# Second layer of a two-layer vision state-space kernel: batch by batch, or stage by stage over all batches

## The chip, the cores and the metric

The kernel runs on one core of a Trainium2 chip. The metric is the device time of one execution in microseconds (us). The engines go by short names: PE is TensorE (matmul; PEld is its weight load), DVE is VectorE, ACT is ScalarE, POOL is GpSimd, SP is SyncE, which issues most DMAs.

## The reference, cut to what matters

The input is `x` with 4 batches of 64x64 positions (L = 4096) and 192 channels, in float32. Two layers follow one another; each adds its result to its input. Both normalise the input by groups, project it to 2x384 channels, run selective scans in four directions over the positions, normalise over channels, multiply by a gate and project back to 192. The change is in the second layer:

```python
xz = x @ W_in
x_val, z = (xz[..., :D_INNER], xz[..., D_INNER:])
xc = conv_general_dilated(xc, conv_w, padding='SAME', feature_group_count=D_INNER)  # 3x3, per channel
xc = silu(xc + conv_b)
y = y1 + y2 + y3 + y4          # scans of rows, rows reversed, columns, columns reversed
y = (y - mu) * rsqrt(var + 1e-05) * gamma + beta
y = y * silu(z)
return y @ W_out

def _ssm_scan(u, ...):         # one direction, 16 states n per channel
    dt = softplus(dt @ W_dt + b_dt)
    log_decay = cumsum(dt * A)
    decay = exp(log_decay)
    h = decay * cumsum(dB_u / (decay + 1e-12))
    return einsum('bldn,bln->bld', h, C_mat) + u * D_param
```

Because of the `1e-12`, a state's output dies away after some steps from where its scan starts. The kernel computes only the first 256 steps of state 0, 128 of states 1 to 3, 64 of states 4 to 7 and 32 of states 8 to 15, in each of the four directions, and tests on the way that this is enough (`alive`); a general layer stands behind it for the case that it isn't, and is not entered here. The rest of y is `4*D*u`, for all 4096 positions.

## The kernel before, in words

`two_layer_vmamba` runs the first layer for each of the four batches (`layer.run(x[b], mid[b])`), then the second layer for each (`layer.run(mid[b], out[b])`). Positions go in 8 tiles of 512 (NCH = 8, LC = 512), inner channels in 3 blocks of 128 (ND = 3). The two layers share `norm` (L442 to L486), `in_proj` (L488, matmuls at L490) and `finish` (from L853). One run of the second layer has three parts.

`project` first normalises (L454 to L482, PE transposes and small DVE work). Then, for each channel block e, ACT copies eight projected tiles into a padded 66x66 plane (`pad`, L993), and each half of the plane (128x2048) is convolved: the middle row of three taps on PE with diagonal weights (L1005), the first tap joined with it from PSUM by DVE in quarters of the half, and five taps (1, 2, 6, 7, 8) on DVE over the whole half (L1023, `acc`). ACT's silu (L1031) writes `u`. GpSimd copies the ends of the plane to `uc` (L1042 rows, L1045 columns), the 512 positions near the four starts and the 512 after these. At last, tile by tile, the gate half of the projection is copied out (L1051) and stored, and `u` is transposed on PE (L1060), multiplied by 4·D on DVE (L1061) and stored to `y` in DRAM.

`scans` works on four items: M (first 128 steps of each direction, states 0 to 3), E (the next 128 steps, state 0), S and Q (64 and 32 steps, states 4 to 7 and 8 to 15). A preparation computes dt (ACT Exp and Ln, POOL L1121 to L1125, DVE L1128), its running sums (L1132 `cum`), dt·u transposed (L1187), and the rows of B and C. Nine steps follow; a step makes 128x1536 values of `h`: `weight` (ACT, Sigmoid of the sums, L1237), `decay` (ACT, Exp, L1250), `b_product` (ACT, L1272), `turn_x` (PE, L1287), `scan` (DVE, L1294 and L1132), `c_product` (POOL, L1310) and, two steps later (LAG = 2), `add_y` (PE, L1328, sums in PSUM) or `ext_y` for E (L1344, L1345). `store` adds M's and E's sums into `y` by accumulating DMAs that POOL issues (L1364, L1367). The order in this part is written out by hand (`manual_schedule`) for PE, ACT, DVE and POOL: each takes its instructions in the order of the text, so a waiting instruction holds all behind it on its engine. Elsewhere a scheduler orders the instructions by their data and by free buffers.

`finish` goes tile by tile: loads of `y`, gate and input; statistics per position (DVE L874), their root (ACT L877, which needs a table of its own), scaling (DVE L880), transposes (PE L887), gamma and beta (ACT L890), the product with silu of the gate (DVE L893), the output matmul (PE L898), the input added (DVE L901), and the store.

Of the kernel before, what the change touches and what calls it, by code (L numbers as in the profile page):

```python
# [23 lines left out]
NX = 64  # L24
# [378 lines left out]
class FirstLayer:  # L403
# [29 lines left out]
    def run(self, src, dst):  # L433
        with self.tc.tile_pool(name="xT", bufs=1) as px:
            self.xT = px.tile([CB, NC2, L], F32, name="xT")
            self.w_in = px.tile([CB, NC2, 2 * DI], F32, name="w_in")
            self.bias = px.tile([128, 2 * ND], F32, name="bias")
            self.project(src)
            self.scans()
        self.finish(src, dst)  # L440
# [412 lines left out]
    def finish(self, src, dst):  # L853
        nc, tc = self.tc.nc, self.tc
        with ExitStack() as ctx:
            pool = lambda name, bufs, **k: ctx.enter_context(tc.tile_pool(name=name, bufs=bufs, **k))
            pl, pw = pool("fl", 3), pool("fw", 2)
# [4 lines left out]
            for t in range(NCH):  # L862
                pos = lambda a: a[t * LC : (t + 1) * LC, :].rearrange("(j p) c -> p j c", p=128)
                yt = pl.tile([128, NJ, DI], F32, name="yt")
                nc.sync.dma_start(yt, pos(self.y_dram))
                zg = pl.tile([128, ND, LC], F32, name="zg")
                nc.sync.dma_start(zg, self.gate[t])
                nc.scalar.activation(zg, zg, AF.Silu)
                xl = pl.tile([128, NJ, CH], F32, name="xl")
                nc.sync.dma_start(xl, pos(src))  # L870
                st = pw.tile([128, NJ, nc.vector.BN_STATS_DIM], F32, name="st")
                mv = pw.tile([128, NJ, 2], F32, name="mv")
                for j in range(NJ):
                    nc.vector.bn_stats(st[:, j, :], yt[:, j, :])  # L874
                    nc.vector.bn_aggr(mv[:, j, :], st[:, j, :])
                rs = pw.tile([128, NJ], F32, name="rs")
                nc.scalar.activation(rs, mv[:, :, 1], AF.Sqrt, bias=self.ln_eps)  # L877
                nc.vector.reciprocal(rs, rs)
                for j in range(NJ):
                    nc.vector.tensor_scalar(  # L880
                        yt[:, j, :], yt[:, j, :], mv[:, j, 0:1], rs[:, j : j + 1], ALU.subtract, ALU.mult
                    )
                v = pw.tile([128, ND, LC], F32, name="v")
                for d in range(ND):
                    vp = pm.tile([128, LC], F32, name="vp")
                    for j in range(NJ):
                        nc.tensor.transpose(  # L887
                            vp[:, j * 128 : (j + 1) * 128], yt[:, j, d * 128 : (d + 1) * 128], self.ident
                        )
                    nc.scalar.activation(  # L890
                        v[:, d, :], vp, AF.Identity, bias=self.beta[:, d : d + 1], scale=self.gamma[:, d : d + 1]
                    )
                nc.vector.tensor_mul(v, v, zg)  # L893
                ot = pw.tile([128, NJ, CH], F32, name="ot")
                for j in range(NJ):
                    op = po.tile([128, CH], F32, name="op")
                    for d in range(ND):
                        nc.tensor.matmul(  # L898
                            op, v[:, d, j * 128 : (j + 1) * 128], w_out[:, d, :], start=(d == 0), stop=(d == ND - 1)
                        )  # L900
                    nc.vector.tensor_add(ot[:, j, :], op, xl[:, j, :])  # L901
                nc.sync.dma_start(pos(dst), ot)


class SecondLayer(FirstLayer):
# [4 lines left out]

    CLASSES = ((0, 1, 2 * SEG), (1, 4, SEG), (4, 8, SEG // 2), (8, 16, SEG // 4))

    def __init__(self, tc, ctx, consts, w, gate, bc_pool, y_dram, alive):
        nc = tc.nc
        self.tc, self.w, self.alive = tc, w, alive
        self.ident, self.group, self.one = consts
        self.gate, self.bc_pool, self.y_dram = gate, bc_pool, y_dram
# [33 lines left out]
    def run(self, src, dst):  # L951
        tc = self.tc
        with tc.tile_pool(name="uc", bufs=1) as pc:
            self.uc = pc.tile([128, 2, ND, LC], F32, name="uc")
            with tc.tile_pool(name="u", bufs=1) as pu:
                self.u = pu.tile([128, ND, L], F32, name="u")
                self.project(src)
            self.scans()
        self.finish(src, dst)


    def project(self, src):
        nc, tc = self.tc.nc, self.tc
        with ExitStack() as ctx:
            pool = lambda name, bufs, **k: ctx.enter_context(tc.tile_pool(name=name, bufs=bufs, **k))
            px, pl, ps = pool("xT", 1), pool("ld", 3), pool("st", 1)
# [3 lines left out]
            pd, pc, pa = pool("dg", 2), pool("pad", 2), pool("acc", 2)  # L970
            dsum = ps.tile([128, DI], F32, name="dsum")
            nc.sync.dma_start(dsum, self.w["D_rows"][0].partition_broadcast(128))
            nc.vector.tensor_scalar_mul(dsum, dsum, float(KD))
            self.xT = px.tile([CB, NC2, L], F32, name="xT")
            self.w_in = ps.tile([CB, NC2, 2 * DI], F32, name="w_in")
            self.bias = bias = ps.tile([128, 2 * ND], F32, name="bias")
            self.norm(src, pl, ps, pt)
            in_proj = lambda e, t: self.in_proj(pm.tile([128, LC], F32, name="pp"), e, t)


            rows = LC // HW
            half = NCH // 2
            for e in range(ND):
                dg = pd.tile([128, 3, 128], F32, name="dg")
                for dx in range(3):
                    nc.vector.tensor_scalar_mul(dg[:, dx, :], self.ident, self.cw[:, e, 3 + dx : 4 + dx])
                pad = pc.tile([128, HW + 2, HW + 2], F32, name="pad")
                nc.gpsimd.memset(pad[:, 0, :], 0.0)  # L988
                nc.gpsimd.memset(pad[:, HW + 1, :], 0.0)
                nc.gpsimd.memset(pad[:, 1 : HW + 1, 0:1], 0.0)  # L990
                nc.gpsimd.memset(pad[:, 1 : HW + 1, HW + 1 : HW + 2], 0.0)
                for t in range(NCH):
                    nc.scalar.activation(  # L993
                        pad[:, 1 + t * rows : 1 + (t + 1) * rows, 1 : 1 + HW],
                        in_proj(e, t).rearrange("p (h w) -> p h w", w=HW),
                        AF.Identity,
                        bias=bias[:, e : e + 1],
                    )
                for q in range(2):
                    acc = pa.tile([128, half * rows, HW], F32, name="acc")  # L1000
                    for t in range(half):
                        cp = pm.tile([128, rows, HW], F32, name="pp")
                        r0 = q * half * rows + t * rows
                        for dx in range(3):
                            nc.tensor.matmul(  # L1005
                                cp,
                                dg[:, dx, :],
                                pad[:, 1 + r0 : 1 + r0 + rows, dx : dx + HW],
                                start=(dx == 0),
                                stop=(dx == 2),  # L1010
                            )
                        nc.vector.scalar_tensor_tensor(
                            acc[:, t * rows : (t + 1) * rows, :],
                            pad[:, r0 : r0 + rows, 0:HW],
                            self.cw[:, e, 0:1],
                            cp,
                            ALU.mult,
                            ALU.add,
                        )
                    r0 = q * half * rows  # L1020
                    for tap in (1, 2, 6, 7, 8):
                        dy, dx = divmod(tap, 3)
                        nc.vector.scalar_tensor_tensor(  # L1023
                            acc,
                            pad[:, r0 + dy : r0 + dy + half * rows, dx : dx + HW],
                            self.cw[:, e, tap : tap + 1],
                            acc,
                            ALU.mult,
                            ALU.add,
                        )  # L1030
                    nc.scalar.activation(  # L1031
                        self.u[:, e, q * half * LC : (q + 1) * half * LC],
                        acc.rearrange("p h w -> p (h w)"),
                        AF.Silu,
                        bias=self.cb[:, e : e + 1],
                    )
            v = self.u.rearrange("p d (h w) -> p d w h", w=HW)
            for r in range(2):
                near, far = r * SEG, (r + 1) * SEG
# [25 lines left out]
    def scans(self):  # L1065
        nc, tc = self.tc.nc, self.tc
        with ExitStack() as ctx:
# [93 lines left out]
            def test(it):  # L1161

                for i, (_, _, n) in enumerate(self.CLASSES):
                    if (n > SEG) != it.r:
                        continue
# [390 lines left out]
```

## Time and profile before

| | |
|---|---|
| median of 3 runs | 11613.56 us (11609.38 to 11620.19) |
| profiled execution, its own time | 11625.22 us |
| its span, first to last instruction | 11623.4 us |
| granted TensorE clock, mean | 0.930 |
| busy in the span | PE 85%, PEld 64%, DVE 84%, ACT 83%, POOL 74% |
| DMA | 1213.58 MB, mean 104 GB/s |
| ACT table loads in the second layer's scans | 8 of Sigmoid (L1237), 1283 ns each |
| second layer | 9916.3 to the end, four batches of about 425.6 us |

The first layer takes 9916 of the 11623 us, so the shares of the whole span describe it more than the second layer. A row of the groups of instructions reads: line, engine, operation, output <- inputs by the program's names, shapes, count, then busy time in us with the mean ns of one, then the idle time before them with what ended it. A row of the timeline reads: start in us, duration, engine, line, operation, names, shape, count, and in brackets the wait before it with what ended it.

### The profile page before, as it was taken

What the parts mean: (1) busy time and instruction counts of PE and PEld (TensorE: products, weight loads), DVE (VectorE), ACT (ScalarE), POOL (GpSimd) and SP (SyncE); (2) the same over time, 40 slices, a digit from 0 to 9 for tenths busy, and PEclk for the clock granted to TensorE, in tenths of its full rate; (3) what the DMA queues carried; (4) which work ended last, traced back from release to release, by engine and by line L of the source; (5) the groups of instructions that cost most, each with busy time, mean ns of one, the idle gap of its engine ahead of it and who ended that gap; (6) DMA issues with size and microseconds to landing.
All of it is one profiled execution on the core that took longest, in us unless ns stands there. A gap on an engine that the chain in (4) does not pass through costs nothing. (4 is left out here: it accounts for less than half of the span.)

```text
span 11623.4 us, 171905 instructions
## 1 busy us (share of the span) xinstructions
PE 9831.9 (85%) x61689; PEld 7403.8 (64%) x61689; DVE 9803.3 (84%) x12067; ACT 9634.3 (83%) x16710; POOL 8590.2 (74%) x2840
## 2 busy tenths in 40 slices
PE   7998888878988888789988888789888887876876
PEld 4776666656776666657766666567766666454454
DVE  4999899957999899849998999679998998666655
ACT  5999999948999999859999999589999998345435
POOL 3999899927999899739998999279998997112112
PEclk8999999988999999989999999889999999887888
DMA  4333343443333343433333444433333344233123
GB/s 124 107 105 99 93 102 97 97 144 113 108 101 95 96 102 97 130 120 109 106 100 93 98 101 98 143 112 110 100 97 96 99 99 125 72 91 126 60 88 124
DMA packets 738067, 1213.58 MB, mean 104 GB/s; under 512 B 48538, under 2 KB 439719, under 8 KB 737204
## 3 DMA queue, kind: packets, MB, share of 16 engines
q1 hardware_dynamic: 732340, 1196.21, 37.0%
q0 software_dynamic: 4864, 6.29, 0.4%
q8 instruction: 490, 8.03, 0.3%
q14 instruction: 373, 3.06, 0.1%
HBM read 927.26 MB, written 275.09 MB: 103 GB/s over the span
## 5 line engine op out<-in xcount | busy, mean ns | idle before, releaser
L738 POOL TENSOR_TENSOR h<-h,bct 128x1536 f32<-128x1536 f32 x2048 | 7065.1, 3473 | 581.0 <-DVE carry L734 481.3
L724 DVE TENSOR_TENSOR_SCAN h<-a,carry,x 128x512 f32<-128x512 f32 x5376 | 6606.0, 1267 | 230.6 <-PE x L716 188.2
L716 PE MATMUL x<-ident,xT 128*128 128x128 f32 x24576 | 4002.5, 287 | 814.5 <-DVE h L724 711.9
L699 ACT ACTIVATE xT<-dtuT,bT 128x384 f32<-128x384 f32 x8192 | 4356.6, 608 | 92.8 <-PE x L716 88.6
L716 PEld LDWEIGHTS x<-ident,xT 128*128 128x128 f32 x24576 | 2804.5, 145 | 2139.3 <-DVE h L724 927.8
L711 ACT ACTIVATE a<-dt,A_log_f 128x512 f32<-128x512 f32 x6144 | 3975.4, 715 | 0.0
L751 PE MATMUL yp<-ident,h 128*128 128x128 f32 x24576 | 3704.7, 277 | 9.2 <-POOL h L738 9.2
L751 PEld LDWEIGHTS yp<-ident,h 128*128 128x128 f32 x24576 | 2945.7, 144 | 78.5 <-issue 62.6
L615 PE MATMUL dp<-xd,w_dtb_f 13*128 13x512 f32 x1536 | 890.4, 663 | 208.5 <-DVE dt L644 207.5
L724 DVE TENSOR_TENSOR_SCAN h<-a,x 128x512 f32<-128x512 f32 x768 | 899.2, 1207 | 193.2 <-PE x L716 116.7
L628 POOL TENSOR_SCALAR wl<-e 128x1536 f32<-128x1536 f32 x128 | 189.5, 1481 | 950.1 <-ACT e L624 791.2
L490 PE MATMUL pp<-xT,w_in 96*128 96x512 f32 x1152 | 544.6, 620 | 0.0
L615 PEld LDWEIGHTS dp<-xd,w_dtb_f 13*128 13x128 f32 x1536 | 238.9, 192 | 453.6 <-DVE dt L644 336.2
L745 PE MATMUL yp<-yold,ident 128*128 128x512 f32 x768 | 442.0, 660 | 72.9 <-DMA yold<-y 72.9
L988 POOL MEMSET pad<- 128x66 f32 x12 | 2.1, 172 | 678.0 <-DVE acc L1023 660.5
L621 ACT ACTIVATE e<-dp 128x512 f32<-128x512 f32 x384 | 225.0, 586 | 309.9 <-DVE dt L644 153.9
L641 POOL TENSOR_TENSOR e<-e,wl 128x1536 f32<-128x1536 f32 x128 | 445.6, 3481 | 0.3
L638 POOL TENSOR_TENSOR e<-e,dt 128x1536 f32<-128x1536 f32 x128 | 443.4, 3464 | 0.3
L898 PE MATMUL op<-w_out,v 128*128 128x192 f32 x1536 | 321.7, 378 | 112.7 <-DVE v L893 112.7
L898 PEld LDWEIGHTS op<-w_out,v 128*128 128x128 f32 x1536 | 307.5, 226 | 125.5 <-DVE v L893 125.5
L734 DVE TENSOR_REDUCE carry<-h 128x3 f32<-128x3 f32 x2048 | 322.7, 158 | 70.4
L490 PEld LDWEIGHTS pp<-xT,w_in 96*128 96x128 f32 x1152 | 222.2, 199 | 248.6 <-issue 243.3
(188 smaller groups left out, 7217.9 us busy)
## 6 DMA issues: line engine op xcount, KB each, us to landing
bct<-xp SPq DMA_DIRECT2D x1024, 512.0 KB, 4.9
y<-du SPq DMA_DIRECT2D x64, 768.0 KB, 5.2
uT<-uT SPq DMA_DIRECT2D x64, 768.0 KB, 4.9
yold<-y SPq DMA_DIRECT2D x64, 768.0 KB, 7.9
gate<-zg SPq DMA_DIRECT2D x64, 768.0 KB, 5.6
y<-yt SPq DMA_DIRECT2D x64, 768.0 KB, 4.2
uT<-uT SPq DMA_DIRECT2D x128, 384.0 KB, 5.1
yold<-y SPq DMA_DIRECT2D x128, 384.0 KB, 5.5
```

The costliest lines, as they stand in the source:

```text
L490: self.tc.nc.tensor.matmul(pp, self.w_in[:, i, e * 128 : (e + 1) * 128], self.xT[:, i, t * LC : (t + 1) * LC], start=(i == 0), stop=(i == ...
L615: nc.tensor.matmul(self.dp[d], w, self.xd[0 : DR + 1, :], start=True, stop=True)
L638: nc.gpsimd.tensor_tensor(self.e, self.e, self.dt, ALU.subtract)
L641: nc.gpsimd.tensor_tensor(self.e, self.e, self.wl, ALU.add)
L699: nc.scalar.mul(xTs[g][:, j, :], it.dtuT[:, j * DI : (j + 1) * DI], it.bT[:, j, n : n + 1])
L711: nc.scalar.activation(as_[g][:, d, :], it.dt[:, d, :], AF.Exp, scale=scale)
L716: nc.tensor.transpose(xs[g, d][:, j * 128 : (j + 1) * 128], xTs[g][:, j, d * 128 : (d + 1) * 128], ident)
L724: nc.vector.tensor_tensor_scan(along(hs[g][:, d, :], it.k), along(as_[g][:, d, :], it.k), along(xs.pop((g, d)), it.k), 0.0 if it.first els ...
L738: nc.gpsimd.tensor_tensor(hs[g], hs[g], bc(cs[g - n % 2][:, n % 2, :], 1, ND), ALU.mult)
L745: nc.tensor.matmul(it.yp[b], ident, yo, start=True, stop=False, skip_group_check=True)
L751: nc.tensor.matmul(it.yp[b][:, i * 128 : (i + 1) * 128], hs[g][:, d, j * 128 : (j + 1) * 128], ident, start=False, stop=n == NS - 1, is_tr ...
L898: nc.tensor.matmul(op, v[:, d, j * 128 : (j + 1) * 128], w_out[:, d, :], start=(d == 0), stop=(d == ND - 1))
```

## The change

- `SecondLayer.run` takes all four batches. Each of its stages goes through all batches before the next stage begins: `project`, `prepare`, `scans`, `finish`. `y` and the gate have a DRAM buffer for each batch, and `uc` goes to DRAM as well.
- `project`: the middle-row taps leave PE. ACT makes taps 0 and 1 (Identity with a scale, 128x2048), POOL adds them, DVE does taps 2 to 8. The normalisation of the next batch is placed after the second channel block of the present one. `uc` is copied by POOL for each half-plane and direction, six copies per half. `4·D·u` comes from a PE matmul of `u` with a diagonal matrix, copied by ACT and stored in blocks of 128 channels (runs of 512 bytes). The gate is stored per channel block.
- `prepare` is new: for M and E of each batch it computes dt, sums and dt·u, cuts S and Q out of M on POOL, and keeps all in DRAM.
- `scans` is one pipeline of 4x9 = 36 steps, with the loads of the next batch's items at its steps 0, 3, 5 and 6. The Sigmoid weights come in two bursts for each batch, five after step 3 and four after step 8. A batch's sums are copied out and stored at step 2 of the next.
- `finish` takes a list of batches: all eight tiles of `y` are loaded and their statistics computed first, with one root for the whole batch; those of the next batch are placed after tile 4. The product with the gate's silu moves from DVE to POOL. The first layer uses this form too, one batch at a time.

The diff, cut:

```diff
...
-    def run(self, src, dst):
...
+    def run(self, batches):
...
+        self.prepare(ucs, chunks)
+        self.scans(chunks, [y for _, _, y, _ in batches])
+        self.finish(batches)
...
+                        nc.scalar.activation(acc, part(0), AF.Identity, scale=weight(0))
+                        nc.scalar.activation(u, part(1), AF.Identity, scale=weight(1))
+                        nc.gpsimd.tensor_tensor(acc, acc, u, ALU.add)
+                        for tap in range(2, 9):
+                            nc.vector.scalar_tensor_tensor(acc, part(tap), weight(tap), acc, ALU.mult, ALU.add)
+                        nc.scalar.activation(u, acc, AF.Silu, bias=self.cb[:, e : e + 1])
...
+                            nc.gpsimd.tensor_copy(to, u[:, row : row + n, :])
...
+                                nc.gpsimd.tensor_copy(to[:, :, q * nh : (q + 1) * nh], wide[:, col : col + n, :])
...
+                                nc.tensor.matmul(
+                                    dq[:, j, :], flat[:, at : at + 128], self.dg[:, e, :], start=True, stop=True
+                                )
+                            du = pl.tile([128, NJ, 128], F32, name="du")
+                            nc.scalar.copy(du, dq)
...
+                    if e == 1 and b + 1 < len(batches):
+                        ready = normed(batches[b + 1][0])
...
+                    burst = {3: range(g + 1, g + 6), 8: range(g + 1, g + 5)}.get(n, ())
...
+                    if n == LAG and b > 0:
+                        end_y(b - 1)
+                        if g < N:
+                            start_y()
...
+                for t in range(NCH):
+                    yt = py.tile([128, NJ, DI], F32, name="yt")
+                    nc.sync.dma_start(yt, pos(y, t))
...
+                        nc.vector.bn_stats(st[:, j, :], yt[:, j, :])
...
-                nc.vector.tensor_mul(v, v, zg)
...
+                    nc.gpsimd.tensor_tensor(v, v, zg, ALU.mult)
...
+                    if t == NCH // 2 and b + 1 < len(batches):
+                        ready = stats(batches[b + 1][2])
...
```

## The prediction, made before the changed kernel ran

> **What bounds the kernel now.** I read first the per-core view (one core, span 11623.4 us, clock 0.930), then the timeline for where the second layer starts: its first statistics begin at 9916.3, and its four batches follow one another at about 425.6 us each. Only this last 1707 us and the output stage of the first layer are touched. So the page's shares over the whole span decide nothing here, and I cut the first batch of the second layer into stages. The columns are the stretch, its length, busy us of PE, PEld, DVE, ACT and POOL, then PE clock, DMA share and GB/s.
>
> ```profile
> 9916.00:9950.00 34.00, 22.63 (x95) 16.18 (x96) 13.86 (x30) 10.79 (x18) 0.00 (x0) 0.57 0.24 70
> 9950.00:10061.00 111.00, 111.00 (x256) 48.89 (x257) 76.34 (x54) 28.29 (x32) 3.38 (x12) 0.98 0.00 0
> 10061.00:10108.00 47.00, 45.96 (x175) 24.62 (x174) 26.13 (x37) 18.55 (x25) 5.38 (x8) 1.00 0.65 245
> 10108.00:10157.00 49.00, 30.62 (x72) 13.71 (x73) 25.93 (x41) 27.20 (x37) 24.84 (x20) 0.61 0.12 40
> 10157.00:10230.00 73.00, 43.27 (x269) 34.71 (x268) 58.57 (x114) 54.55 (x119) 28.66 (x9) 0.79 0.10 27
> 10230.00:10270.00 40.00, 17.65 (x133) 14.88 (x130) 2.65 (x8) 7.50 (x6) 13.80 (x20) 0.77 0.57 128
> 10270.00:10342.00 72.00, 50.11 (x289) 47.17 (x289) 54.68 (x145) 39.52 (x47) 0.00 (x0) 0.84 0.71 236
> ```
>
> The rows are norm, convolution, gate with D·u, scan preparation, scan steps, the scan's tail with its stores, and output. Convolution is bound by PE (111.00 of 111.00). The tail of 40 us has no busy engine: it is a chain of waits. The other stages have no full engine either. Then the durations, from the groups of instructions with forms apart:
>
> ```profile
> L898 PE MATMUL op<-w_out,v 128*128 128x192 f32 x1536 | 321.7, 378 | 112.7 <-DVE v L893 112.7
> L1023 DVE SCALAR_TENSOR_TENSOR acc<-pad,conv_w_s,acc 128x2048 f32<-128x2048 f32 x120 | 281.1, 2351 | 1.3
> L893 DVE TENSOR_TENSOR v<-v,zg 128x1536 f32<-128x1536 f32 x64 | 112.1, 1752 | 28.5 <-ACT v L890 27.7
> L1132 DVE TENSOR_TENSOR_SCAN cum<-keep_s,dt 128x256 f32<-128x256 f32 x24 | 45.3, 1927 | 0.4
> ```
>
> Last the timeline, for what the scan's tail waits on. POOL issues the accumulating stores of the E chunk one by one, each waiting for the one before to land, and the last h·C product stands behind them:
>
> ```profile
> 10228.30 1.06 POOL L1364 DMA_DIRECT2D y<-yte  x1 [0.61 <-ACT yte L1345]
> 10232.69 1.70 POOL L1367 DMA_DIRECT2D y<-yte  x2 [3.33 <-DMA y<-yte]
> 10237.02 0.90 POOL L1364 DMA_DIRECT2D y<-yte  x1 [2.63 <-DMA y<-yte]
> 10240.84 1.68 POOL L1367 DMA_DIRECT2D y<-yte  x2 [2.92 <-DMA y<-yte]
> 10241.96 4.00 POOL L1310 TENSOR_TENSOR h<-h,bct 128x1536 f32<-128x1536 f32 x1
> ```
>
> So one store set holds POOL for about 14.2 us (10228.3 to 10242.5).
>
> **What the Trainium skill says.** (1) "SBUF — State Buffer", section Who interferes with whom: a DVE instruction with two SBUF inputs and a GpSimd instruction that reads SBUF share a read port, and the second to issue waits until the first is done. The trace agrees. The 128x256 scan takes 674 ns in the main loop (L1132 h) but 1927 on average where POOL works beside it (row above). In the timeline:
>
> ```profile
> 10132.06 3.67 POOL L1123 TENSOR_TENSOR e<-e,dt 128x1536 f32<-128x1536 f32 x1
> 10133.13 6.92 DVE L1132 TENSOR_TENSOR_SCAN cum<-keep_s,dt 128x256 f32<-128x256 f32 x2
> 10135.81 3.68 POOL L1125 TENSOR_TENSOR e<-e,wl 128x1536 f32<-128x1536 f32 x1
> 10140.66 1.27 DVE L1132 TENSOR_TENSOR_SCAN cum<-keep_s,dt 128x256 f32<-128x256 f32 x2
> ```
>
> Two scans take 6.92 beside POOL and 1.27 alone; two products of 3.42 and two scans of 0.63 make 8.1, and 8.0 pass from 10132.06 to 10140.05. The port is handed over whole, at no extra price. (2) "GPSIMD Engine Reference", section 4.1 Engine selection: two-input elementwise work is about twice as slow as on VectorE; the trace has 3510 against 1752 ns for 128x1536. (3) "ScalarE: Activation LUTs", section What ACT_TABLE_LOAD costs: about 1.28 us a load plus a drain; the load is 1283 ns here, and no drain is seen after it.
>
> **The change, part by part.** P, S, C, O are its four stages.
>
> *P, norm to gate, now for all batches in a row.* Before: 34+111+47 = 192 per batch, 768. After, PE has 192 projection passes at 0.461 (88.5), 192 D·u passes of 128 columns, about 0.15 each (29), and norm (22.6): 140 per batch; the 144 convolution passes (62.4) are gone. ACT has 24 pad copies and 24 gate copies at 0.69 (33), 12 Identity passes of 128x2048, not in the trace, bounded by the silu of that size, 2.0 (24), 6 silus (12), 24 du copies at 0.59 (14), norm 11: about 95, hidden. DVE has 7 taps of 2.351 for each half-plane (taps read two SBUF inputs), 6 half-planes: 98.7. With norm (11) and small work (2), 112. On top come GpSimd's holds of the shared port: six adds of 128x2048, 3473×2048/1536 = 4.63 each, of which five fall between taps (23); and 36 copies to uc, 12 at 0.40 and 24 of 64x32 pieces, no row, nearest the 404 ns of 128x128, taken 0.29 (between 0.2 and 1.5), about 10 between taps. That makes **145 per batch**. DVE is now the bound, just above PE. At each turn of a batch pads come only after the last silu: bias products 4, four pads 5, ACT taps and add 9, in all 19 us, three times. Start: norm 34 and 16 to the first tap. End: 12. SP issues 24 D·u and 24 gate stores per batch instead of 8 and 8, and the next batch's norm loads stand behind them; the same bytes moved in 47 us before and have 145 now, so nothing, with 10 per batch as the cost if the loads come late. P = 50+3×145+134+57+12 = **about 690, −78**. Bounds: 560 if the port costs DVE nothing (PE's 4×140), 830 if each half-plane pays as in the rival below.
>
> *S, prepare, all batches ahead of the scans.* Before 49 per batch (196). After, the chain of one batch is read from the same rows: xd to exp 8.7 with a table load, POOL 10 (2×1.5+2×3.5), delta and sums 6.3, then for the second chunk wl, dt and two products behind POOL's part copies (15), sums 7, products and transposes to dtuT 6: 53. The next batch's Abs stands behind this batch's dtuT copies on ACT, so 7+4×53 = **219, +23**. Chunks stored to DRAM, 6.5 MB per batch, take 20 us at 332 GB/s (236/0.71 of the output row) and lie under the 53. Bounds 170 (if batches overlap) and 260.
>
> *C, one pipeline of 36 steps.* Before 73+40 per batch (452). ACT's work per batch is 26.3 weights (105.3/4), 21.8 decays, 19 b products, 2.4 copies, 5.1 table loads: 74.6. The drain and fill, paid four times now, are paid once. But the E store still holds POOL 14.2 us, and in the pipeline it starts just after the weights of the ninth step: product 8 waits, add_y 8 follows about 9 later on PE, and ACT's copy of ytm stands ahead of the next burst: about 12 of stall. Period 86.5. Load 6, ramp 54, three periods 259: 320 to the last batch's final steps, with the y loads of O starting meanwhile, 47 after that. C = **320**. Bounds: 284 (no stall), 368 (twice the stall).
>
> *O, output for four batches.* Before 72 each (288). After: 76 to 78 us from the end of those 320 for the first y loads, behind the last stores, and all eight statistics; first tile 16; then 32 tiles. A tile moves 2.36 MB, 7.1 us at 332 GB/s. PE needs 5.6 to 6.8. DVE has 1.75 less (row L893), but the product goes to POOL at 3.5 and holds the port there: about 7.3. So O = 78+16+32×7.25+6 = **332, +44**. The skill, (4) "DMA: Bandwidth & Descriptors", section Where 436 GB/s comes from, gives about 358 GB/s as the HBM limit of a core; the trace shows 236 at share 0.71, and I use that. C and O together take 652 against 740: −88.
>
> *First layer's output, four times.* Its stage is 84 us (9832 to 9916). All eight tiles' statistics now go first: PE starts near +29 instead of +10, then runs 5.8 to 6.4 per tile. **+6 each, +24**; bounds −10 (POOL's product frees DVE) and +45.
>
> Table loads: in O and in the first layer's output 100 become 17, in prepare 16 come new; off the bounding engine in both, so nothing. If ACT were the bound, 83×1.28 = 106.
>
> Sum for the second layer: 690+219+320+332 = 1561 against 1707 (3 more than my rounded stages add up to), −146; with +24, −122. The profiled execution took 11625.2 by its own time (span 11623.4), so 11503; the median of the runs is 11.7 below the profiled one: **11492 us**. What is late next: in P DVE, in C ACT with POOL's stall, in O the DMA.
>
> **The rivals.** (R1) Faster: DVE doesn't wait for GpSimd in P, which is PE-bound at 560. −130 more: 11362. Against it stands the 1927 ns row. (R2) Slower than before: the port in P. Each half-plane has seven GpSimd instructions (one add, six copies), and DVE and GpSimd take turns. If a half-plane costs 30 us instead of 24, because each of the seven holds the port 0.9 longer than its own length or the 64x32 copies take 1.3 to 1.5, P grows by 24×6 = 144: 11636. It decides from 5.1 us per half-plane upward (122/24). For it: the copies' strided form has no row. Against it: the 8.0 us hand-over shows no extra price. (R3) Faster: POOL's store stall is not on the path of C, period 74.6, −36: 11456. (R4) No change: the pipeline does not do what it says, because loads of the next batch come late or batches of S and O wait for DRAM; the gain of C and O goes (88) and a little of P: 11590 to 11620.
>
> **How the numbers follow.** Forecast 0.54, R1 0.10, R3 0.10, R4 0.08, R2 0.18 (with all other sums that end slower). A measurement here can tell about 0.2% (23 us) from no change. Faster: 0.54+0.10+0.10 = 0.74; same 0.08; slower 0.18. The range reaches from 11380, which leaves out most of R1 (0.07), to 11620, which takes in R4 and leaves out 0.13 of R2. Its width is that of P's bounds for the most part.
>
> **What would show it.** Right: taps of 128x2048 near 2.35 with one or two per half-plane near 4 to 7; a half-plane every 24 us; prepare with a period near 53; sigmoid bursts 86 apart; output tiles 7.2 apart at a DMA share near 1; first statistics 29 ahead of PE in the first layer's output. Wrong: half-planes at 30 or more (R2) or P ending at 560 (R1), a period of 75 (R3), scan groups waiting on DMA loads (R4).

## The result, and the profile after

The changed kernel takes 11564.99 us (median of 4 runs, 11548.21 to 11574.44) against 11613.05 for the kernel before in the same comparison: a ratio of 0.9956, with a 95% interval of 0.9939 to 0.9974. It is faster, by 48 us. The prediction said 11492, faster by 122. The direction was right, and the time lies in the range; the gain is 0.4 of the forecast.

The profiled execution of the changed kernel took 11574.44 us (span 11572.7), 50.8 less than that of before. First the stages, in the view by stretches (columns as in the prediction). The rows are norm; the first batch of convolution and gate; the first batch of prepare; a period of the scan pipeline; then the last stores, the statistics, and the first two stretches of the output stage.

```profile
9948.00:9998.00 50.00, 34.99 (x120) 21.66 (x121) 13.52 (x26) 17.45 (x25) 0.90 (x8) 0.69 0.38 112
9998.00:10160.00 162.00, 123.41 (x474) 72.39 (x473) 123.91 (x68) 89.03 (x110) 85.07 (x54) 0.86 0.34 111
10633.00:10687.00 54.00, 34.64 (x68) 14.68 (x68) 10.52 (x32) 19.25 (x23) 26.75 (x24) 0.59 0.31 115
...
10983.00:11068.00 85.00, 56.82 (x388) 45.52 (x386) 52.34 (x91) 71.89 (x146) 41.20 (x21) 0.84 0.48 121
11240.00:11268.00 28.00, 8.80 (x66) 7.42 (x63) 1.69 (x3) 7.39 (x6) 5.18 (x6) 0.68 0.73 208
11268.00:11300.00 32.00, 7.11 (x37) 6.55 (x38) 26.51 (x91) 4.44 (x7) 7.98 (x2) 0.61 0.79 290
11300.00:11366.00 66.00, 47.98 (x273) 44.99 (x272) 54.08 (x142) 30.34 (x34) 30.63 (x8) 0.89 0.71 238
11366.00:11433.00 67.00, 52.78 (x302) 49.14 (x302) 47.39 (x123) 31.79 (x37) 26.71 (x8) 0.87 0.77 255
```

In a convolution batch of 162 us PE and DVE are both busy for 124 and ACT for 89: no engine is full. The output stage has no full engine either, and DMA is at 0.71 to 0.77. Both are chains of waits. The groups of instructions of the changed kernel name what is waited for:

```profile
L912 PE MATMUL op<-w_out,v 128*128 128x192 f32 x1536 | 302.0, 364 | 105.9 <-POOL v L907 104.3 <-DVE ot L915 1.5
L907 POOL TENSOR_TENSOR v<-v,zg 128x1536 f32<-128x1536 f32 x64 | 238.2, 3742 | 422.2 <-ACT v L904 380.3 <-ACT zg L888 35.8 <-PE vp L901 6.0
L1056 DVE SCALAR_TENSOR_TENSOR acc<-pad,conv_w_s,acc 128x2048 f32<-128x2048 f32 x168 | 446.2, 2702 | 139.1 <-POOL acc L1054 138.8
L1054 POOL TENSOR_TENSOR acc<-acc,u 128x2048 f32<-128x2048 f32 x24 | 134.6, 5608 | 130.9 <-ACT u L1053 130.9
L1053 ACT ACTIVATE u<-pad,conv_w_s 128x2048 f32<-128x2048 f32 x24 | 47.9, 1997 | 65.8 <-POOL uc L1067 61.2 <-PE pp L490 4.6
L1067 POOL COPY uc<-u 128x64 f32<-128x64 f32 x96 | 103.7, 1107 | 0.0
L1064 POOL COPY uc<-u 128x128 f32<-128x128 f32 x48 | 102.7, 2139 | 181.6 <-ACT u L1057 181.6
L939 DVE TENSOR_TENSOR_SCAN cum<-keep_s,dt 128x256 f32<-128x256 f32 x24 | 14.4, 666 | 0.0
```

PE's output matmuls waited for DVE's product before (112.7 in both layers) and wait about as long for POOL's now. The taps are longer (2702 against 2351 ns), and DVE stands idle for 139 us until POOL's add. POOL itself stands idle for 131 us before its adds, until ACT's second tap (L1053) is done. POOL's copies of 128x128 (columns before, rows now) take 2139 ns against 404. In exchange the running sums in prepare (`cum`) have the port for themselves: 666 ns against 1927.

E's stores still stand ahead of a batch's last product. After them three products follow in one run, and PE's sums (L1343) wait for the first of these:

```profile
11057.71 0.91 POOL L1377 DMA_DIRECT2D y<-yte  x1 [8.06 <-ACT yte L1361]
11061.87 1.69 POOL L1380 DMA_DIRECT2D y<-yte  x2 [3.25 <-ACT a L1267]
11066.22 0.90 POOL L1377 DMA_DIRECT2D y<-yte  x1 [2.66 <-ACT a L1267]
11070.99 1.68 POOL L1380 DMA_DIRECT2D y<-yte  x2 [3.87 <-DMA y<-yte]
11072.12 10.77 POOL L1325 TENSOR_TENSOR h<-h,bct 128x1536 f32<-128x1536 f32 x3
11076.17 3.42 PE L1343 MATMUL yp<-ident,h 128*32 128x128 f32 x16 [5.62 <-POOL h L1325]
```

The timeline gives all stages to a microsecond, and the same instants can be read in each experiment. "Start" is the first transpose of the second layer's norm; "conv" runs from there to the last gate copy; "prepare" to the last copy of dt·u; "scans" from the first to the last product of x; "output" from the first output matmul to the last sum.

| run | median us | start | conv | prepare | scans | output |
|---|---|---|---|---|---|---|
| changed kernel | 11565.0 | 9952.6 | 680.0 | 237.1 | 323.2 | 268.2 |
| e1 product on DVE | 11445.3 | 9888.9 | 676.9 | 235.3 | 324.4 | 211.1 |
| e2 four v | 11567.3 | 9946.7 | 680.1 | 236.4 | 324.9 | 273.8 |
| e3 first layer's old form | 11530.4 | 9909.1 | 678.4 | 235.1 | 326.3 | 268.3 |
| e4 store late | 11540.1 | 9935.5 | 679.7 | 236.9 | 300.3 | 263.5 |
| e5 no add | 11541.1 | 9940.6 | 662.3 | 236.5 | 326.2 | 265.8 |
| e6 copies on ACT | 11543.3 | 9944.2 | 656.9 | 235.5 | 325.2 | 268.7 |
| e7 e5 and e6 | 11445.7 | 9941.2 | 565.8 | 234.8 | 324.3 | 262.0 |
| e8 ytm apart | 11560.2 | 9943.7 | 676.4 | 237.0 | 325.2 | 279.4 |
| e9 six PSUM banks | 11578.6 | 9942.1 | 674.6 | 238.2 | 324.3 | 283.6 |
| e10 prepare in pairs | 11560.8 | 9950.9 | 679.9 | 229.1 | 325.6 | 267.3 |
| e13 PE's order | 11507.3 | 9926.9 | 677.0 | 238.3 | 321.8 | 235.6 |
| e14 no add, borders on DVE | 11428.4 | 9939.2 | 538.8 | 244.8 | 323.9 | 261.7 |
| e16 borders on DVE | 11534.1 | 9935.0 | 663.7 | 231.5 | 324.7 | 268.6 |

The start varies from run to run: in the eight runs that leave all of `finish` as changed (e4 to e8, e10, e14, e16) it lies between 9935.0 and 9950.9, mean 9941. So the changed kernel's profile, with 9952.6, is late by some 11 us, and differences of ten microseconds in the median of a run are read from the stages here.

### The profile page after: what moved, and what is told of

The parts are those of the page before. It is cut to its first block, busy times and chain, and to the rows that moved or that the text cites. A ratio compares the mean times of both kernels' runs of the same rounds, so it can differ in the third digit from the quotient of the medians.

```text
span 11572.7 us, 172113 instructions
## 1 busy us (share of the span) xinstructions
PE 9631.2 (83%) x61497; PEld 7333.9 (63%) x61497; DVE 9684.7 (84%) x11675; ACT 9692.9 (84%) x16786; POOL 9137.6 (79%) x3024
## 5 line engine op out<-in xcount | busy, mean ns | idle before, releaser
L907 POOL TENSOR_TENSOR v<-v,zg 128x1536 f32<-128x1536 f32 x64 | 238.2, 3742 | 422.2 <-ACT v L904 380.3
L1056 DVE SCALAR_TENSOR_TENSOR acc<-pad,conv_w_s,acc 128x2048 f32<-128x2048 f32 x168 | 446.2, 2702 | 139.1 <-POOL acc L1054 138.8
```

What stands on the lines that cost most here:

```text
L1056: nc.vector.scalar_tensor_tensor(acc, part(tap), weight(tap), acc, ALU.mult, ALU.add)
```

## The experiments

The main theory after the result was that GpSimd costs in two places where the sum had it hidden: in the output stage its product lies on PE's path, and in the convolution its queue delays DVE. The rivals were DMA (output) and the price of the port for DVE alone (convolution).

**Output stage.** e1 puts the product back:

```diff
-                    nc.gpsimd.tensor_tensor(v, v, zg, ALU.mult)
+                    nc.vector.tensor_mul(v, v, zg)
```

> The changed kernel with the product of v and the gate's silu put back on VectorE, in both layers. Theory (the output stage is paced by its chain: PE's output matmuls of two tiles, then ACT's copies of v, then GpSimd's product, with PE idle while GpSimd multiplies; two buffers of v): 3.42 on the path becomes 1.75, so a pair of tiles takes about 12.8 instead of 14.5 us. In the second layer's 32 tiles 27 us less, in the first layer's 4 times 8 tiles up to 25 less: about 11520 in all, against 11565. Rival (DMA paces the tiles, share 0.71 to 0.77): pairs stay at 14.5 and the time stays within 10 us of 11565. Second rival (VectorE becomes the bound with statistics, scaling and sums): pairs at 16 or more, some 25 us slower.

Measured: 11445.3, ratio 0.985 (0.9834 to 0.9867) to the kernel before. The output stage falls from 268.2 to 211.1 (6.6 a tile), and the second layer starts at 9888.9, 27 us ahead of where it started before the change (9915.9). The gain of 120 is over twice what the theory gave: the pairs of tiles took 16.8 on average (268.2/16), not the 14.5 of a steady stretch, and now take 13.2. The first rival is out: DMA did not set the pace. Now it is nearly full, with 327 GB/s at a share of 0.96 in this stretch:

```profile
11226.00:11292.00 66.00, 57.43 (x358) 53.56 (x356) 64.88 (x170) 38.15 (x43) 0.00 (x0) 0.95 0.96 327
```

DVE is as full (64.9 of 66), and which of the two sets the pace now is not shown. Why POOL's product cost so much was asked next. e2 gives v four buffers (`bufs=4` on its tile); e9 adds six PSUM banks for the transposes and two for the sums (pools `fm` and `fo`).

> The changed kernel with four buffers of v instead of two, the product left on GpSimd. Theory (the two buffers tie ACT's next v to the output matmuls of two tiles before, so PE idles during the product): with four the product of one pair runs beneath PE's matmuls of another, and a tile comes to PE's 6.1 to 6.8 us: 32 tiles save 45 to 60 us in the second layer and the first layer's output some 30, about 11470. Rival (DMA paces): tiles at 7.2 and over, 11530 or more. Rival (PSUM: the four vp buffers tie it as well): no change, 11565.

> The changed kernel with four v buffers as in the run with four v, and PSUM of the output stage cut otherwise: six banks for the transposes (vp), two for the sums (op); the product on GpSimd. What is open: four v buffers alone changed nothing. Theory A (PE's transposes of the next pair have no PSUM bank until ACT has emptied the last, so PE still waits for GpSimd's product): with six banks two tiles of transposes fit ahead, and the 32 tiles take 215 to 245 us instead of 268 to 274; about 11520. Theory B (the order that the scheduler gives PE, transposes of two tiles and then output matmuls of two tiles, with the product between, is the cause, and it stays): 260 to 275, 11565. Theory C (two op banks now hold PE back by VectorE's sums): 280 or more.

Measured: 11567.3 and 11578.6, output 273.8 and 283.6. More buffers or other banks do not help; with six banks and two it is 10 longer than in e2. Both theories of the kind "not enough buffers" fell. The timeline of the changed kernel shows what is left:

```profile
11384.83 2.58 PE L901 MATMUL vp<-ident,yt 128*128 128x128 f32 x22
11385.36 2.79 ACT L904 ACTIVATE v<-vp,beta_s,gamma_s 128x512 f32<-128x512 f32 x4 [1.35 <-PE vp L901]
11386.28 6.83 POOL L907 TENSOR_TENSOR v<-v,zg 128x1536 f32<-128x1536 f32 x2 [7.70 <-ACT v L904]
11389.78 9.75 PE L912 MATMUL op<-w_out,v 128*128 128x192 f32 x48 [2.36 <-POOL v L907]
```

PE does the transposes of two tiles, then stands until the first product is done, then the output matmuls of two tiles (48). The scheduler chose this order. e13 writes PE's order by hand and leaves the product on POOL:

```diff
+            with tc.manual_schedule(engines={nc.tensor.engine}):
...
+                        if late:
+                            sums(*late)
+                        late = (v, xl, dst, t)
```

(`sums` holds the output matmuls, their sums and the store of one tile; v has three buffers.)

> The changed kernel with the output stage's order on PE written out by hand: the transposes of tile t+1, then the output matmuls of tile t; three buffers of v; the product stays on GpSimd. Theory B (the scheduler's order, two tiles at a time, leaves PE idle during the products): a product of 3.42 now lies under the output matmuls of 4.9 of the tile before, a tile comes to 6.6 to 7.3, the 32 tiles to 215 to 235 instead of 268, and the first layer's output gains too: 11470 to 11510. Theory D (GpSimd and VectorE take turns at the port, and VectorE's scaling is what waits): 255 or more, about 11560.

Measured: 11507.3 (ratio 0.9902, 0.9886 to 0.9919), output 235.6, start 9926.9. So PE's order alone gives 33 of e1's 57 us. The whole stage in the changed kernel, in e13 and in e1:

```profile
11297.80:11566.00 268.20, 202.38 (x1123) 189.91 (x1123) 162.64 (x426) 114.15 (x129) 112.24 (x31) 0.85 0.70 230
11268.30:11503.90 235.60, 183.55 (x1129) 176.83 (x1129) 163.68 (x425) 114.51 (x129) 107.33 (x31) 0.90 0.78 261
11226.20:11437.30 211.10, 180.96 (x1118) 169.90 (x1117) 186.02 (x463) 113.87 (x129) 0.00 (x0) 0.94 0.87 293
```

PE waits 53 us for the product in the changed kernel, 44 in e13 and 7 in e1. So the order removed only 9 us of this wait. A larger part of what it gained is that the same matmuls and transposes kept PE busy for 183.6 us at a granted clock of 0.90, instead of 202.4 at 0.85; why the clock differs was not tested. The two gains overlap: under the order by hand the product's place is still worth 32 (235.6 against the 203.1 of e15 below, which also loads y earlier), and with the product on DVE the order is worth 11 (203.1 against 213.8 in e12).

**First layer.** e3 calls the old output stage there, and only there.

```diff
-        self.finish([(src, dst, self.y_dram, self.gate)])
+        self.finish_one(src, dst)
```

> The changed kernel with the first layer's output stage in the old form (tile by tile, product on VectorE); the second layer as changed. Theory: the second layer's start, which moved from 9915.9 to 9952.6, goes back by 35 us, and the time by as much: 11530. Rival (the first layer lost by something else than its output stage, such as where its buffers lie): the second layer's start stays near 9950 and the time near 11565.

Measured: 11530.4, start 9909.1. So the new form cost the first layer 32 us against the mean start of 9941 (44 against this profile's), and by e1 that is the product: with it on DVE, "statistics first" gains 20 (9888.9 against 9909.1; e11 and e12 below start at 9883.7 and 9889.2).

**Convolution.** e5 gives DVE tap 1, so that the add on POOL goes; e6 moves the copies to uc to ACT; e7 does both.

```diff
-                        nc.scalar.activation(u, part(1), AF.Identity, scale=weight(1))
-                        nc.gpsimd.tensor_tensor(acc, acc, u, ALU.add)
-                        for tap in range(2, 9):
+                        for tap in range(1, 9):
...
-                            nc.gpsimd.tensor_copy(to, u[:, row : row + n, :])
+                            nc.scalar.copy(to, u[:, row : row + n, :])
```

(The second part, with the same edit on the column copies, is e6's.)

> The changed kernel with tap 1 of the convolution on VectorE (eight taps there), so that neither ACT's second tap nor GpSimd's add of 128x2048 is left. Theory (VectorE waits 5.8 us for that add at each half-plane and again where the add holds the shared port): a tap of 2.35 more, but 5.8 of waiting and up to 4.6 of holding less; a half-plane goes from 27.1 to 21 to 23 us, limited by PE's 140 a batch, and the four batches of norm to gate from 680 to 570 to 600: about 11470. Rival (the copies to uc on GpSimd are what delays, and the add only stands behind them): 24 to 26 a half-plane, about 11540. Rival (VectorE is full): 2.35 more a half-plane, 11620.

> The changed kernel with the copies to uc (six for each half-plane) on ACT instead of GpSimd; the add stays on GpSimd. Theory (GpSimd's copies, stretched to 2.14 and 1.11 us by turns for the port, stand ahead of the next add): VectorE's wait for the add shrinks from 5.8 to 1 to 3 us and its taps come down from 2.70 towards 2.5; ACT gets some 0.3 each, 36 of them, 11 a batch, from 89 of 162. Norm to gate 680 to about 600 to 630: about 11500. Rival (the add alone is the cost): 660 and more, 11550.

> The changed kernel with both edits: eight taps on VectorE and the copies to uc on ACT, so GpSimd touches nothing of the convolution but the pad's borders. Theory: taps at 2.33 throughout, a half-plane at PE's or VectorE's 19 to 22 us, norm to gate 540 to 580, about 11450. It is also the test of the prediction's case in which the port costs nothing. Rival (ACT, with 95 a batch and a chain of pads, taps and silus, holds the half-planes apart): 620 or more, about 11510.

Measured: conv 662.3, 656.9 and 565.8. Alone the edits give 18 and 23, both near their rivals and far from their theories; together they give 114. Each hides the other. In e5 the taps are at 2343 ns, so the copies left on POOL do not lengthen them, and still the planes come late. The timeline of e5 shows how:

```profile
10007.04 45.33 DVE L1054 SCALAR_TENSOR_TENSOR acc<-pad,conv_w_s,acc 128x2048 f32<-128x2048 f32 x20
...
10016.01 36.51 POOL L1062 COPY uc<-u 128x128 f32<-128x128 f32 x1 [78.23 <-ACT u L1055]
...
10058.82 0.21 POOL L1037 MEMSET pad<- 128x64 f32 x1
...
10059.07 2.00 ACT L1052 ACTIVATE acc<-pad,conv_w_s 128x2048 f32<-128x2048 f32 x1 [29.01 <-POOL pad L1037]
```

DVE runs twenty taps without a gap. A copy on POOL that takes 0.3 us elsewhere lasts 36.51: it comes to no turn before the run ends. Behind it stand the border memsets of the next plane, and ACT waits 29 us for these before it can start that plane (97.7 over the four batches). e14 is e5 with the four memsets on DVE, the 36 copies of a batch still on POOL; e16 moves the memsets alone.

```diff
-                    nc.gpsimd.memset(pad[:, 0, :], 0.0)
+                    nc.vector.memset(pad[:, 0, :], 0.0)
```

> The changed kernel with eight taps on VectorE (no add on GpSimd) and the pad's border memsets on VectorE; the copies to uc stay on GpSimd. Theory (GpSimd's copies starve beside VectorE's back-to-back taps, and the next plane's border memsets stand behind them on GpSimd's queue, so ACT starts the plane late): with the memsets off that queue norm to gate falls from 662 to 565 to 590: about 11455. Rival (the copies hold back VectorE's taps or the buffers of u): 640 to 665, 11530.

> The changed kernel with nothing but the pad's border memsets on VectorE. Theory M (the memsets are late by themselves, and with them the plane): norm to gate from 680 to 590 to 630, about 11490. Theory A (with the add on GpSimd's queue each half-plane waits there anyway, and the memsets only stand in the same line): 660 to 680, 11550.

Measured: conv 538.8 in e14 and 663.7 in e16. In e14 POOL's copies are about as slow as in the changed kernel, and the convolution no longer waits for them:

```profile
L1054 DVE SCALAR_TENSOR_TENSOR acc<-pad,conv_w_s,acc 128x2048 f32<-128x2048 f32 x192 | 442.0, 2350 | 29.0 <-ACT acc L1052 28.6
L1065 POOL COPY uc<-u 128x64 f32<-128x64 f32 x96 | 136.8, 1453 | 0.0
L1062 POOL COPY uc<-u 128x128 f32<-128x128 f32 x48 | 93.2, 1941 | 339.6 <-ACT u L1055 339.6
```

So what counted was less DVE's price for the port than what waits for POOL: the taps for the add (for this half-plane), and ACT for the memsets behind starved copies (for the next plane). Taking one off leaves the other: in e6, where POOL has no copies, DVE still waits 112.6 us for the add, and in e16 128.4. e16's 16 us are near Theory A's, but not for the reason that it gives. The add did not stand behind copies on POOL's queue: in the changed kernel it starts 0.1 us after ACT's second tap ends in 21 of 24 half-planes, and 1.7 us after it in the other three. What it costs comes from its place in the chain of ACT, POOL and DVE. The copies delay that chain from another side, for ACT's second tap waits 61.2 us for buffers of u that they still read (row L1053 above). e5 takes away this tap together with the add, so what each of the two is worth alone is not shown. Prepare takes 244.8 in e14, 8 more than in the changed kernel, which gives back a part; why was not looked into.

**Scans.** e4 issues E's stores after the product of the same step.

```diff
-                if b == ND - 1:
-                    store(it.y, flat[g][2], SEG)
...
                         c_product(g)
+                    if g >= LAG and g - LAG < N and flat[g - LAG][0].name == "E":
+                        store(flat[g - LAG][0].y, flat[g - LAG][2], SEG)
```

> The changed kernel with E's accumulating stores issued after the h times C product of the ninth step instead of ahead of it (the same work in another order on GpSimd's queue). Theory (the stores hold that product for 14 us, add_y for it comes late on PE, and ACT waits for it before the next burst of weights): the period of a batch in the scans falls from 85.6 towards ACT's sum of 74.6, three periods and the last tail give 30 to 40 us: about 11530. Rival (the stores then hold the next batch's products just as long, four h buffers notwithstanding): period 83 to 87, 11565.

Measured: scans 300.3 instead of 323.2; the period, from one batch's burst of five weights to the next one's, is 77.7 instead of 85.4. The stall is what the prediction said, at 7.7 instead of 12.

e8 takes ytm from a pool that stays open into `finish`.

> The changed kernel with the buffer of the last batch's sums (ytm) in a pool that stays open into the output stage. Theory (the first load of y waits for the memory of that buffer, which the last accumulating stores hold until 11261): the loads of y begin with the last scan step, near 11240, and all behind comes 15 to 22 us sooner: about 11545. Rival (the loads wait for other memory of the scans, or for the stores themselves): no change, 11565.

Measured: the loads of y start 17.4 us after the last scan step instead of 42.3, so it was that memory the first of them waited for. But from that scan step to the last output sum 341.9 pass against 345.4: the output stage, which POOL sets, takes it back (279.4).

**Prepare.** e10 puts another batch's chunk between M and E (order M0, M1, E0, E1, and one buffer more).

> The changed kernel with prepare's chunks in the order M of batch 0, M of 1, E of 0, E of 1, then the same for 2 and 3, and four buffers instead of three where they are needed. Theory (prepare's 54 a batch is a chain in which E waits for M's sums and the engines are half idle, PE 36 of 54 the fullest): with another batch's chunk between, prepare falls from 237 towards PE's 150 to 190; about 11510. Rival (the order on ACT and GpSimd is what holds, and stays): 225 to 240, 11560.

Measured: 229.1, 8 less, as its rival said. That hardly stands out: e16, which leaves prepare as it is, has 231.5, and e12 and e15, which have the pairs, have 239.7 and 239.3. The theory fell; what holds the chunks apart was not found.

**Together.** e11 is e1, e7 and e4; e12 adds e8 and e10; e15 adds PE's order by hand; e17 takes e1, e14, e4, e8 and that order.

> The changed kernel with the edits that gained, together: the product on VectorE (both layers), eight taps on VectorE and the copies to uc on ACT, E's stores after the ninth step's product. If the stages are independent, the stage savings add: norm to gate 114, scans 23, output 57, and the first layer's output 55 to 60 of the profiled 37 lost: about 11310 (11295 to 11330). Rival (a gain in one stage is taken back by the next): above 11350.

> The same with prepare in pairs of batches and ytm in a pool that stays open. Theory: whatever prepare in pairs saves alone (20 to 80) and up to 15 from loads of y that start earlier, now that the output stage can use them: 11220 to 11290. Rival: the earlier loads give nothing, as alone, and prepare does not overlap: 11310.

> The kernel of five edits with PE's order in the output stage written out by hand as well, product on VectorE. If the output stage there is bound by DMA (share 0.96 at 327 GB/s in the run with the product on VectorE), nothing is gained: 11295 to 11315. Rival (PE's order still costs some): up to 20 us in the second layer and 15 in the first: 11270 to 11290.

> The changed kernel with the product on VectorE, eight taps and the border memsets on VectorE and the copies to uc left on GpSimd, E's stores after the ninth step's product, ytm in a pool that stays open, PE's order in the output stage by hand, prepare as changed. If the stage gains add: the run with all edits and the order (11285) less the 20 us between norm to gate of 559 and 539: 11255 to 11275. Rival (the next stage waits for something else): 11280 or more.

Measured: 11308.3, 11305.5, 11285.3 and **11260.6** (11258.95 to 11263.09). The last has a ratio of 0.969 (0.9674 to 0.9706) to the kernel before; conv is 535.1, prepare 244.6, scans 302.7, output 203.7. The savings of stages add (e11 was expected at 11310, e17 at 11255 to 11275). e15 is 20 below e12, as its rival said: the output stage with the product on DVE was not held by DMA alone. e12 gained nothing by prepare (239.7), and 12 us between prepare's end and the last output sum by the earlier loads of y.

## Why the prediction was wrong

Its sum, against the profile of the changed kernel:

| step | predicted | measured | miss |
|---|---|---|---|
| first layer's output | +24 | +36.7 (typical run +25) | +12.7 |
| P, norm to gate | 690 | 680.0 | −10 |
| S, prepare | 219 | 237.1 | +18.1 |
| C and O, scans and output | 652 | 702.9 | +50.9 |

The misses add to 71.7 (the forecast was 122, the profiled gain 50.7 in span).

**The step that failed is O's 7.25 us per tile.** The prediction took the largest of three engines' sums (DMA 7.1, PE 5.6 to 6.8, DVE 7.3), and had POOL's 3.5 only as a hold of the port. It measured 268.2/32 = 8.4, some 36 us over 32 tiles. e1 shows that the stage does run at 6.6 a tile when the product is DVE's, and e13 that PE's order by hand, with the product still on POOL, gets more than half of the difference. (The sums of 7.1 for DMA and 7.3 for DVE were thus too high as well, and hid a part of the miss.) The change put a slower engine into a chain (ACT, product, PE) whose links the scheduler did not overlap; the row that the prediction itself showed (L898 waits 112.7 for DVE's v) said that PE waits for this very product. The other part of C and O is that the y loads began 393 us after prepare's end, not 367: the first of them waited for the last stores' buffer (369 in e8, without that wait). The prediction names these stores ahead of the loads, but gives the wait no figure of its own. The first output matmul then followed 35 us later instead of 47, which gave half of that back.

**P was right in size by luck.** It had 33 us of port holds per batch on DVE, and 19 at each turn from one batch to the next. The taps are longer by only (2702−2343)×42 = 15. DVE's wait for POOL's add comes to 139/4 = 35 per batch: 26 to 28 of it at the turn, and a further 8 inside the batch, where the prediction had no wait. The sum of about 50 came out as forecast, in other parts. R1, "the port costs DVE nothing, P is 560", measured 566 in e7 and 539 in e14: PE's 140 a batch was a little high. R2, a dearer port for DVE, did not come: the copies are five times dearer on POOL, not on DVE.

**S was mis-sized**: from one E to the next 57.4 pass, not 53; which link of the chain is longer was not found. **C's stall was right**, 7.7 instead of 12, and the period 85.4 as the 86.5 forecast. **The first layer** lost what was forecast in a typical run, but for another reason: not the late start of PE (statistics first gains, by e1 against e3) but the product on POOL, for which a bound of −10 had been noted.

Two small sums of the prediction do not come out: 4, 5 and 9 at a batch's turn make 18, not 19 (3 us in P), and C with twice the stall is 60+3×98.6 = 356 by its own terms, not 368. Neither changes the forecast.

## What to carry to other kernels

When elementwise work moves to a slower engine, add its duration to the chain between the engines around it, and look in the profile for who waits for its result; an engine's sum of busy time says nothing on it. When an engine's queue is starved, list all that stands behind the starved instruction, small memsets for the next stage too, and the buffers that it still reads, and expect that taking away one of two waiters shows little: take both.

## What the runs showed of the hardware that was not expected

A GpSimd copy of 128x128, 0.29 us alone, lasted 36.51 us beside a run of twenty VectorE taps without a gap (2.27 each), and ended 0.15 us after the run. Before the change GpSimd and VectorE took turns at the port (the 8.0 us of the prediction's last timeline), and the Trainium skill ("SBUF — State Buffer", section Who interferes with whom) has the second engine blocked for the whole instruction of the first, so a wait of one tap, 2.3 us, had been expected. Here it was a run of them; the measurement decides. e5 has such a wait once in each of its four batches (36.46 to 36.51 us), e14 once in all (36.45), and the changed kernel one per batch of 10.3 to 11.6 us beside runs of five or six taps. It is no rule for taps without a gap, though: in e14 three copies in a row got a turn each, one per tap, beside six such taps, as the page has it.

```profile
10117.52 13.81 DVE L1054 SCALAR_TENSOR_TENSOR acc<-pad,conv_w_s,acc 128x2048 f32<-128x2048 f32 x6
10119.97 2.36 POOL L1062 COPY uc<-u 128x128 f32<-128x128 f32 x1
10122.27 4.64 POOL L1065 COPY uc<-u 128x64 f32<-128x64 f32 x2
```

What decides between the two was not found. ACT does the same copies in 0.30 us, and the memsets take 0.11 on VectorE against 0.15 to 0.25 on GpSimd.
